# The last pair of graphs in two halves, and the last attentions in a shorter schedule: a graph network on one core

## Chip, core and metric

The kernel runs on one core of a Trainium2 chip. The metric is the device time of one execution in microseconds. The kernel before takes 2255.85 us, the median of three runs (2254.88 to 2256.64).

## What is computed

Sixty-four graphs of 256 nodes with 256 features each. Three GRU layers over the graph (layer 0 of the reference), a residual with a layer norm, then one attention layer with a residual and a layer norm. Everything is fp32.

```python
A = (adj != 0)
h = x
for i in range(3):
    m = einsum('bnd,de->bne', h, weight[i])
    aggr = einsum('bst,bsd->btd', A, m)
    h = gru_cell(aggr, h, w_ih, w_hh, b_ih, b_hh)   # r, z: sigmoid; n: tanh
x = layernorm(x + h)
Wh = x @ W
e = leaky_relu(s1[:, :, None] + s2[:, None, :], 0.2)  # s1, s2: Wh @ a[:F], Wh @ a[F:]
attn = softmax(where(adj > 0, e, -9e15), axis=2)
x = layernorm(x + attn @ Wh)
```

## The kernel before

**Tiles.** Graphs are taken in 32 pairs (`NP`). A pair has 512 node columns (`GN`), so a gate's result fills one PSUM bank of 128x512, and there are eight banks in one pool. The state `hT` is kept transposed, two tiles of 128 features by 512 nodes. To keep fp32 accuracy, an operand of a gate is cut into an upper part H, a rest L and a cross term D (`upper`, `lower`, `cross`, L126 to L134), and a product is a sum over such pieces in two banks, `pga` and `pgb` (L360 to L377): ScalarE evicts the first, VectorE adds the second.

**Blocks.** One layer of one pair is a block: `front` (L290) prepares the pieces of h (`hH`, `hL`, `hD`) and of the aggregation (`hi`, `lo`, then `pa`, then `aH`, `aL`, `aD`); `gates` (L356) makes eight products of r, n, z and t, four for each half `e` of the features, and the elementwise steps of the GRU: the sigmoids and the tanh on ScalarE (L386), two multiplications, a subtraction and an addition on GpSimd (L394, L395, L400, L404), the last addition into `hT` on VectorE (L407). A block's gates are 72 matmuls of 512 columns. The three layers of different pairs are interleaved: with each turn, a new pair starts layer 0, the pair before it does layer 1, and the one before that does layer 2 (L549 to L551). The last six blocks are (31,0), (30,1), (29,2), then (31,1), (30,2), then (31,2).

**Order of the work.** Each engine runs its instructions in the order in which the program issues them. That order is set by a clock of ticks: `at(t, step)` files a step, and `tick()` after every six gate matmuls (L370, L376) runs what has come due, so the steps of the front of the next block and of the attention of earlier pairs fall between the gate matmuls. A block has twelve ticks. The front's steps have fixed offsets, `CLOSE` or `LOOSE` (L545, L546). After the last block the loop at L591 runs the remaining steps in order of their ticks.

**Attention.** After a pair's third layer `attention` (L441) files its steps at offsets up to 72 ticks: load x back (`vT`, 5), join with h (14), transpose and copy (15 to 18), statistics for the first layer norm (23), power on GpSimd (26), shift (28), projection `pwh` (31 to 34) and its spreading with the norm's factor onto `s1`, `s2` and `wh` (32 to 35, half on ScalarE, half on VectorE), transposes of the row scores `s` (36), scores on ScalarE (37), mask (38), maximum (39), exponentials (46, 47), first norm applied to `v` (49, 50), transposes of the weights (53), combine `po` (57, 58), add (58, 59), second norm (61 to 70) and the store (72). The exponential and the sigmoid with tanh sit in different function tables of ScalarE, and the compiled program has a table load wherever one follows the other: 61 in all.

**Rooms.** `room` (L255) gives the large attention tiles: from a pool of their own up to pair 29, and from the tags of the gate pieces (`hH`, `hD`, `aH`, `aD`) for pairs 30 and 31. The tiles `hi` and `lo` have one buffer each, and the s2 tile of the attention uses the buffer of `hi0`. A copy of x (transposed) is put away in DRAM (`stash`, L311) and loaded again for the attention.

Of the kernel before, what the change touches and what calls it, by code (L numbers as in the profile page):

```python
# [17 lines left out]
P = 128  # L18
# [7 lines left out]
def kernel(  # L26
# [91 lines left out]

    def nodes(t, d):

        return t.rearrange("p g c d -> p (g c) d")[:, :, d * P:(d + 1) * P]
# [130 lines left out]

    pairs = {}

    def room(kind, shape, p):  # L255


        name = f"{kind}_{p}"
        if p < NP - 2:
            return late.tile(shape, F32, tag=kind, name=name, bufs=2 if kind == "v" else 1)  # L260
        tag = {"v": "hH", "vT": "hD", "wh": "aH", "sc": "aD"}[kind]
        return work.tile(shape, F32, tag=tag, name=name)

    def to_T(src, dst, d):

        pt = bank("pt")
        for k in range(K):
            nc.tensor.transpose(pt[:, k * P:(k + 1) * P], src[:, k // C, k % C, d * P:(d + 1) * P], ident)  # L268
        after(1, lambda: evacuate(dst[:, d, :], pt))

    def from_T(hT, d):
        pt = bank("pt")
        for k in range(K):
            nc.tensor.transpose(pt[:, k * P:(k + 1) * P], hT[:, d, k * P:(k + 1) * P], ident)  # L274
        return pt

    def begin(p):

        s = pairs[p] = Pair()
        s.x, s.adj = loaded.pop(p), loaded_adj.pop(p)  # L280
        s.A = work.tile([P, G, C, N], F32R, tag="A", name=f"A_{p}", bufs=3)
        nc.vector.tensor_scalar(s.A, s.adj, 0.0, None, op0=ALU.not_equal)
        s.hT = work.tile([P, C, GN], F32, tag="hT", name=f"hT_{p}", bufs=4)

# [5 lines left out]
    def front(p, i, t, pace):  # L290

        nm = f"{p}_{i}"
        hi, lo, src = [None] * C, [None] * C, [None] * C

        def turn(d):
            s = pairs[p]
            if i == 0:
                src[d] = nodes(s.x, d)
                to_T(s.x, s.hT, d)
            else:  # L300
                src[d] = from_T(s.hT, d).rearrange("p (k n) -> p k n", k=K)

        def split(d):
            hi[d] = work.tile([P, K, P], F32R, tag=f"hi{d}", name=f"hi{d}_{nm}", bufs=1)
            nc.scalar.copy(hi[d], src[d])

        def rest(d):
            lo[d] = work.tile([P, K, P], F32R, tag=f"lo{d}", name=f"lo{d}_{nm}", bufs=1)
            lower(nc.gpsimd if i == 0 else nc.vector, lo[d], src[d], hi[d])

        def stash():  # L311
            s = pairs[p]
            s.far = far.tile([P, C, GN], F32, tag="xT", name=f"xT_{p}")
            nc.sync.dma_start(s.far, s.hT)
        if i == 0:
            at(t + pace[0][1] + 2, stash)

        def h_upper():
            s = pairs[p]
            s.hc = pieces(work, [P, C, GN], nm, "h")  # L320
            upper(flat(s.hc[0]), flat(s.hT))

        def h_lower():
            s = pairs[p]
            lower(nc.gpsimd, flat(s.hc[1]), flat(s.hT), flat(s.hc[0]))

        def h_cross():
            s = pairs[p]
            cross(flat(s.hc[2]), flat(s.hT), flat(s.hc[0]))

        def aggregate(d):
            s = pairs[p]
            if d == 0:
                s.ag = pieces(work, [P, C, GN], nm, "a")
            pt = src[d] = bank("pa")
            for g in range(G):
                todo = [(h[d], c) for c in range(C) for h in (hi, lo)]
                for n, (h, c) in enumerate(todo):
                    nc.tensor.matmul(pt[:, g * N:(g + 1) * N], h[:, g * C + c, :], s.A[:, g, c, :],  # L339
                                     start=(n == 0), stop=(n == len(todo) - 1))  # L340

        def a_upper(d):
            upper(pairs[p].ag[0][:, d, :], src[d])

        def a_rest(d):
            H, Lo, Di = [t[:, d, :] for t in pairs[p].ag]
# [9 lines left out]
    def gates(p, i, lags):  # L356

        s = pairs[p]

        def product(dst, o, parts, bias=None):  # L360
# [5 lines left out]
            step = len(todo) // len(parts)  # L366
            for n, (pt, w, m, d) in enumerate(todo):
                nc.tensor.matmul(pt, w[:, d, o * P:(o + 1) * P], m[:, d, :],  # L368
                                 start=n in (0, ends + 1), stop=n in (ends, len(todo) - 1))
                if (n + 1) % step == 0 and n + 1 < len(todo):  # L370
# [5 lines left out]
            tick()  # L376
            nc.vector.scalar_tensor_tensor(dst, b, -1.0 / U, dst, op0=ALU.mult, op1=ALU.add)  # L377

        for e in range(C):
            nm = f"{p}_{i}_{e}"  # L380

            def temp(tag, bufs=2):
                return work.tile([P, GN], F32, tag=tag, name=f"{tag}_{nm}", bufs=bufs)
# [4 lines left out]
            hid, inp = (whh, s.hc), (wc[i], s.ag)  # L388
            bo = [b_sum[:, e:e + 1], b_sum[:, C + e:C + e + 1]]
            r, n, z, t = temp("r", 1), temp("n", 3), temp("z"), temp("t")  # L390
            h = s.hT[:, e, :]
# [4 lines left out]

            product(r, e, [hid, inp])
            after(1, lambda r=r, b=bo[0]: gate(r, AF.Sigmoid, b))
            product(n, 2 * C + e, [hid], bh[:, 2 * C + e:2 * C + e + 1])
            after(2, lambda r=r, n=n: nc.gpsimd.tensor_mul(n, n, r))  # L400
            product(z, C + e, [hid, inp])
            after(2, lambda z=z, b=bo[1]: gate(z, AF.Sigmoid, b))
            product(t, 2 * C + e, [inp])
            after(1, lambda n=n, t=t: nc.gpsimd.tensor_add(n, n, t))  # L404
# [4 lines left out]
    def layer_norm(v, name, t, then=None):  # L409
# [10 lines left out]
        def power():  # L420
            nc.gpsimd.tensor_scalar(rs, mv[:, :, 1], EPS, None, op0=ALU.add)
            nc.gpsimd.tensor_tensor(rs, rs, half, ALU.pow)

        def shift():
            nc.vector.scalar_tensor_tensor(nm, mv[:, :, 0], -1.0, rs, op0=ALU.mult, op1=ALU.mult)
# [5 lines left out]
        for k in range(K):  # L431
            at(t[0] + k // 2, lambda k=k: stats(k))
        at(t[1], power)
        at(t[2], shift)
        for k in range(K):
            at(t[3] + k // 2, lambda k=k: apply(k))
# [4 lines left out]
    def attention(p, t):  # L441

        s = pairs[p]
        pts = {}

        def again():
            s.vT = room("vT", [P, C, GN], p)
            nc.sync.dma_start(s.vT, s.far)
        at(t + 5, again)
        at(t + 14, lambda: nc.vector.tensor_add(flat(s.vT), flat(s.vT), flat(s.hT)))  # L450

        def back(d):
            if d == 0:
                s.v = room("v", [P, G, C, D], p)
            pts[d] = from_T(s.vT, d)
        for d in range(C):
            at(t + 15 + d, lambda d=d: back(d))
            at(t + 17 + d, lambda d=d: nc.vector.tensor_copy(
                nodes(s.v, d), pts[d].rearrange("p (k n) -> p k n", k=K)))
        at(t + 18, lambda: setattr(s, "rs", layer_norm(s.v, f"a_{p}", (t + 23, t + 26, t + 28, t + 49))))  # L460

        def project(k):
            if k == 0:
                s.wh = room("wh", [P, G, C, D], p)
                s.s1 = work.tile([P, K], F32, tag="s1", name=f"s1_{p}")
                s.s2 = work.tile([P, K, P], F32, tag="hi0", name=f"s2_{p}", bufs=1)
            pts[k] = bank("pwh")
            for d in range(C):
                nc.tensor.matmul(pts[k][:, :D + 2], s.vT[:, d, k * P:(k + 1) * P], gw[:, d, :],  # L469
                                 start=(d == 0), stop=(d == C - 1))  # L470

        def spread(k):
            rs = s.rs[:, k:k + 1]
            for dst, src in ((s.s1[:, k:k + 1], pts[k][:, D:D + 1]),
                             (s.s2[:, k, :], pts[k][:, D + 1:D + 2].to_broadcast([P, P])),
                             (s.wh[:, k // C, k % C, :], pts[k][:, :D])):
                if k < 2:
# [3 lines left out]
        for k in range(K):  # L481
            at(t + 31 + k, lambda k=k: project(k))
            at(t + 32 + k, lambda k=k: spread(k))

        def rows():
            pts[0] = bank("s2")
            for k in range(K):
                nc.tensor.transpose(pts[0][:, k * P:(k + 1) * P], s.s2[:, k, :], ident)  # L488

        def scores():  # L490
            s.sc = room("sc", [P, K, N], p)
            for k in range(K):
# [130 lines left out]
```

## Time and profile before

| what | value |
| --- | --- |
| median of three runs | 2255.85 us |
| profiled execution | 2255.94 us |
| its span, first to last instruction | 2254.2 us |
| granted TensorE clock, mean | 0.991 |
| TensorE busy | 2205.3 us, 98% of the span |
| VectorE, ScalarE, GpSimd busy | 1627.0, 1494.6, 1496.7 us |
| TensorE busy in the first 60 us | 45.4 us |
| last gate matmul ends (start of the row transposes behind it) | 2189.24 us |
| last ScalarE row ends | 2250.3 us |

The profile is of one execution; its time is 1.7 us above its span. Busy time counts overlapping rows once. TensorE's matmuls are pipelined, so a matmul's own duration (about 0.4 us for 512 columns) is longer than the distance from one to the next; the chain view, which gives the pieces of the path that ended last, has the distances (four matmuls in 0.93 us). An idle time with an arrow names what the engine waited for.

### The profile page before, as it was taken

The numbers are of one execution on the slowest core, as the hardware profiler recorded it, in microseconds if no ns is written. First come the engines' busy times: TensorE is split into PE (matmuls) and PEld (weight loads), VectorE is DVE, ScalarE is ACT, GpSimd is POOL, SyncE is SP. The second block draws the span as 40 slices with busy tenths as digits, with TensorE's granted clock in tenths as the row PEclk, the third lists the DMA queues.
The fourth block names the chain that finished last, engine by engine and source line by source line (L and its number), as shares of the span: only waits on it lengthen the run. The fifth ranks groups of instructions, "written<-read, shape, count | busy, mean of one in ns | idle before, by whom it ended". The sixth has DMA issues, their size and how long they took to land.

```text
span 2254.2 us, 31118 instructions
## 1 busy us (share of the span) xinstructions
PE 2205.3 (98%) x10980; PEld 1839.0 (82%) x10980; DVE 1627.0 (72%) x2856; ACT 1494.6 (66%) x2771; POOL 1496.7 (66%) x1084
## 2 busy tenths in 40 slices
PE   7999999999999999999999999999999999999985
PEld 5788888888888888888888888888888888888874
DVE  4767777777767777767777767777767777767775
ACT  4556667666667666667666677666677666677664
POOL 5777666676666676666667666667666667666661
PEclk9999999999999999999999999999999999999997
DMA  3001011100011101011101011101011101010000
GB/s 112 29 29 38 28 39 48 47 31 36 34 42 48 47 29 38 30 46 47 47 29 37 29 47 47 48 29 38 29 48 47 47 29 38 29 47 29 20 28 28
DMA packets 62650, 88.50 MB, mean 39 GB/s; under 512 B 2784, under 2 KB 54240, under 8 KB 62496
## 3 DMA queue, kind: packets, MB, share of 16 engines
q1 hardware_dynamic: 60704, 84.68, 10.7%
q8 instruction: 87, 1.43, 0.3%
q10 hardware_dynamic: 1616, 1.57, 0.2%
q14 instruction: 67, 0.55, 0.1%
q0 software_dynamic: 176, 0.27, 0.1%
HBM read 52.96 MB, written 33.55 MB: 38 GB/s over the span
## 4 chain that ended last, share of the span: by engine, by line
PE 95%; DVE 1%; ACT 1%; POOL 1%; issue 1%; DMA 1%; SPq 0%; POOLq 0%; ACTq 0%; DVEq 0%
PE pga L368 47%; PE pgb L368 23%; PE pa L339 8%; PE po L525 5%; PE pwh L469 5%; PE pt L274 4%; PE pt L268 1%; PE pt L517 1%; DMA adj<-in_adj_dram 1%; PE s L488 1%; PE pw L229 0%; ACT v L429 0%; DVE sc L502 0%; DVE st_b L417 0%; POOL wc2L_wc L145 0%
## 5 line engine op out<-in xcount | busy, mean ns | idle before, releaser
L394 POOL TENSOR_TENSOR t<-hT,n 128x512 f32<-128x512 f32 x192 | 255.0, 1328 | 534.3 <-ACT n L386 534.2
L368 PE MATMUL pga<-hH,whhH_whh 128*128 128x512 f32 x1152 | 397.4, 426 | 0.0
L368 PE MATMUL pgb<-hD,whhD_whh 128*128 128x512 f32 x1152 | 361.9, 395 | 0.3 <-DVE hD L134 0.3
L368 PE MATMUL pga<-hL,whhL_whh 128*128 128x512 f32 x1152 | 362.0, 395 | 0.0
L404 POOL TENSOR_TENSOR n<-n,t 128x512 f32<-128x512 f32 x192 | 251.8, 1311 | 114.2 <-DVE t L377 101.2
L377 DVE SCALAR_TENSOR_TENSOR r<-pgb,r 128x512 f32<-128x512 f32 x192 | 131.8, 686 | 254.0 <-PE pgb L368 188.5
L400 POOL TENSOR_TENSOR n<-n,r 128x512 f32<-128x512 f32 x192 | 306.2, 1595 | 0.6 <-DVE n L377 0.4
L395 POOL TENSOR_TENSOR t<-t,z 128x512 f32<-128x512 f32 x192 | 263.1, 1370 | 15.0
L368 PEld LDWEIGHTS pgb<-hD,whhD_whh 128*128 128x128 f32 x1152 | 216.3, 188 | 52.6 <-DVE hD L134 0.8
L368 PEld LDWEIGHTS pga<-hL,whhL_whh 128*128 128x128 f32 x1152 | 216.7, 188 | 51.4
L373 ACT ACTIVATE r<-pga 128x512 f32<-128x512 f32 x192 | 115.2, 600 | 216.0 <-PE pga L368 206.2
L375 ACT ACTIVATE n<-pga,bh 128x512 f32<-128x512 f32 x192 | 131.7, 686 | 164.6 <-PE pga L368 164.5
L131 POOL TENSOR_TENSOR hL<-hT,hH 128x1024 fp32r<-128x1024 f32 x96 | 230.6, 2402 | 7.1 <-ACT hH L128 7.1
L368 PEld LDWEIGHTS pga<-hH,whhH_whh 128*128 128x128 f32 x1152 | 193.9, 190 | 20.8
L339 PE MATMUL pa<-A,hi 128*128 128x256 f32 x768 | 200.4, 293 | 0.0
L373 ACT ACTIVATE z<-pga 128x512 f32<-128x512 f32 x192 | 114.7, 597 | 128.7 <-PE pga L368 128.7
L339 PE MATMUL pa<-A,lo 128*128 128x256 f32 x768 | 192.7, 283 | 4.3 <-POOL lo L131 4.3
L377 DVE SCALAR_TENSOR_TENSOR t<-pgb,t 128x512 f32<-128x512 f32 x192 | 131.8, 686 | 78.3 <-ACT t L373 72.3
L377 DVE SCALAR_TENSOR_TENSOR z<-pgb,z 128x512 f32<-128x512 f32 x192 | 131.9, 687 | 73.7 <-ACT z L373 60.9
L131 DVE TENSOR_TENSOR aL<-pa,aH 128x512 fp32r<-128x512 f32 x192 | 131.6, 685 | 55.4 <-ACT aH L128 55.4
L128 ACT ACTIVATE aH<-pa 128x512 fp32r<-128x512 f32 x192 | 115.1, 600 | 78.5 <-PE pa L339 78.5
L377 DVE SCALAR_TENSOR_TENSOR n<-pgb,n 128x512 f32<-128x512 f32 x192 | 131.8, 686 | 43.7 <-ACT n L375 39.3
(133 smaller groups left out, 5439.6 us busy)
## 6 DMA issues: line engine op xcount, KB each, us to landing
x<-in_x_dram SPq DMA_DIRECT2D x32, 512.0 KB, 4.0
adj<-in_adj_dram SPq DMA_DIRECT2D x32, 512.0 KB, 4.0
xT<-hT SPq DMA_DIRECT2D x32, 512.0 KB, 2.6
vT<-xT SPq DMA_DIRECT2D x32, 512.0 KB, 4.8
out_dram<-v SPq DMA_DIRECT2D x32, 512.0 KB, 2.9
w_n<-in_L_gnn_weight_dram ACTq DMA_DIRECT2D x3, 256.0 KB, 10.4
rows_hH<-in_L_gnn_w_hh_dram SPq DMA_DIRECT2D x1, 512.0 KB, 5.5
rows_aH<-in_L_gnn_w_ih_dram ACTq DMA_DIRECT2D x1, 512.0 KB, 6.0
```

Source lines behind the costliest of these rows:

```text
L128: nc.scalar.activation(dst, src, AF.Copy, scale=1.0 - 2.0 ** -13)
L131: eng.tensor_sub(dst, src, hi.bitcast(F32))
L339: nc.tensor.matmul(pt[:, g * N:(g + 1) * N], h[:, g * C + c, :], s.A[:, g, c, :], start=(n == 0), stop=(n == len(todo) - 1))
L368: nc.tensor.matmul(pt, w[:, d, o * P:(o + 1) * P], m[:, d, :], start=n in (0, ends + 1), stop=n in (ends, len(todo) - 1))
L373: nc.scalar.activation(dst, a, AF.Copy, scale=1.0 + U)
L375: nc.scalar.activation(dst, a, AF.Identity, scale=1.0 + U, bias=bias)
L377: nc.vector.scalar_tensor_tensor(dst, b, -1.0 / U, dst, op0=ALU.mult, op1=ALU.add)
L394: nc.gpsimd.tensor_sub(t, h, n)
L395: nc.gpsimd.tensor_mul(t, t, z)
L400: after(2, lambda r=r, n=n: nc.gpsimd.tensor_mul(n, n, r))
L404: after(1, lambda n=n, t=t: nc.gpsimd.tensor_add(n, n, t))
L469: nc.tensor.matmul(pts[k][:, :D + 2], s.vT[:, d, k * P:(k + 1) * P], gw[:, d, :], start=(d == 0), stop=(d == C - 1))
```

## The change

- A class `Unit` stands for a whole pair or one graph of it; `front`, `gates`, `layer_norm` and `attention` take a unit, and their column ranges come from it. Pairs 0 to 30 are whole units. Pair 31 is two units, 31g0 and 31g1, each with 256 columns. They share `hT`, `A`, the mask and the DRAM copy of x; each has its own pieces and its own attention.
- The last blocks become (31g0,0), (31g1,0), (30,1), (29,2), then (31g0,1), (31g1,1), (30,2), then (31g0,2), (31g1,2).
- A tick is now counted by columns, so that a half block has six ticks. While a half block runs, the front of the next block has the offsets `SHORT`, which fit into six ticks, for a whole pair too; half blocks have shorter lags for tanh, blend and the last addition.
- The attention's offsets become a table; its entries are, in order: again, join, back, v, stats, power, shift, apply, project, rows, scores, mask, max, exp, turn, combine, stats2, power2, shift2, apply2. Up to pair 27 it is the old one (`EVEN`); pair 28 has `BRISK` (56 ticks), pairs 29, 30 and both halves of 31 have `FAST` (35 ticks). With the last two, `s2` lies in the buffer of x.
- `room` takes the gate pieces' tags for pair 31 alone; pair 30 uses the attention's own pool.
- The store of x to DRAM is issued in `h_upper`, in the same tick as before, one issue for each half of pair 31.

```diff
-    def room(kind, shape, p):
-        name = f"{kind}_{p}"
-        if p < NP - 2:
+    def room(kind, shape, u):
+        name = f"{kind}_{u.name}"
+        if u.p < NP - 1:
             return late.tile(shape, F32, tag=kind, name=name, bufs=2 if kind == "v" else 1)
...
         def h_upper():
+            if i == 0:
+                nc.sync.dma_start(u.cols(u.pair.far), u.cols(u.pair.hT))
...
-                nc.tensor.matmul(pt, w[:, d, o * P:(o + 1) * P], m[:, d, :],
+                nc.tensor.matmul(u.bank(pt), w[:, d, o * P:(o + 1) * P], u.col(m, d),
                                  start=n in (0, ends + 1), stop=n in (ends, len(todo) - 1))
-                if (n + 1) % step == 0 and n + 1 < len(todo):
+                done[0] += u.n1 - u.n0
+                step = done[0] % (3 * C * GN) == 0
+                if step and n + 1 < len(todo):
                     tick()
...
     CLOSE = (5, 5, 5, 7, 8, 8), (6, 6, 7)
+    SHORT = (0, 1, 1, 3, 4, 4), (3, 3, 4)
     LOOSE = (2, 3, 4, 6, 7, 8), (5, 8, 10)
+    EVEN = 5, 14, 15, 17, 23, 26, 28, 49, 31, 36, 37, 38, 39, 46, 53, 57, 61, 64, 66, 70
+    BRISK = 5, 14, 15, 17, 19, 21, 23, 32, 23, 28, 29, 30, 31, 33, 37, 41, 45, 48, 50, 54
+    FAST = 2, 5, 6, 7, 9, 10, 12, 22, 14, 18, 19, 20, 20, 22, 25, 27, 30, 31, 33, 33
...
+    units = [Unit(p, 0, G) for p in range(NP - 1)]
+    ends = [Unit(NP - 1, g, g + 1) for g in range(G)]
     blocks = []
     for turn in range(NP + L - 1):
-        blocks += [(turn - i, i) for i in range(L) if 0 <= turn - i < NP]
+        if turn >= NP - 1:
+            blocks += [(u, turn - NP + 1) for u in ends]
+        blocks += [(units[turn - i], i) for i in range(L) if 0 <= turn - i < NP - 1]
...
-            front(np_, ni, clock[0], CLOSE if n and np_ == blocks[n - 1][0] else LOOSE)
+            front(nu, ni, clock[0], CLOSE if n and nu is blocks[n - 1][0] else LOOSE if u.whole else SHORT)
...
-        gates(p, i, (2, 3, 5) if n + 2 >= len(blocks) or blocks[n + 2][0] == p else (4, 5, 10))
+        close = n + 2 < len(blocks) and blocks[n + 2][0] is u or n + 1 < len(blocks) and not blocks[n + 1][0].whole
+        gates(u, i, (1, 2, 4) if not u.whole else (2, 3, 5) if close else (4, 5, 10))
         if i == L - 1:
-            attention(p, clock[0])
+            attention(u, clock[0], EVEN if u.p < NP - 4 else BRISK if u.p < NP - 3 else FAST)
```

## The prediction

> **What bounds the kernel now.** I read the page first, then the busy time by stretches of the last 80 us, then the chain and the timeline there.
>
> ```profile
> span 2254.2 us, 31118 instructions
> PE 2205.3 (98%) x10980; PEld 1839.0 (82%) x10980; DVE 1627.0 (72%) x2856; ACT 1494.6 (66%) x2771; POOL 1496.7 (66%) x1084
> ```
>
> TensorE (PE) is the bound. Of its 48.9 us of idle time the start has about 14.5. The stretches (columns: length, PE, PEld, DVE, ACT, POOL busy, granted PE clock, DMA share, GB/s) show where the rest is:
>
> ```profile
> 2150.00:2175.00 25.00, 24.77 (x125) 20.62 (x124) 21.96 (x44) 12.83 (x21) 15.96 (x12) 1.00 0.06 22
> 2175.00:2190.00 15.00, 14.68 (x67) 11.84 (x65) 8.07 (x16) 9.35 (x20) 9.28 (x9) 1.00 0.03 11
> 2190.00:2200.00 10.00, 1.09 (x8) 0.86 (x8) 7.80 (x16) 7.50 (x19) 4.87 (x4) 0.75 0.28 88
> 2200.00:2210.00 10.00, 8.88 (x40) 8.22 (x41) 5.13 (x12) 2.08 (x7) 2.14 (x2) 0.74 0.01 2
> 2220.00:2230.00 10.00, 4.44 (x14) 3.14 (x15) 5.38 (x11) 9.23 (x29) 0.00 (x0) 0.50 0.15 52
> 2240.00:2254.20 14.20, 3.34 (x9) 2.31 (x8) 3.91 (x13) 3.06 (x7) 1.27 (x2) 0.62 0.21 74
> ```
>
> Up to 2190 PE is full. Then comes a drain in which no engine is full and PE's granted clock falls to between 0.50 and 0.75 in the stretches shown. The chain has its pieces:
>
> ```profile
> 2188.78 0.46 PE pgb L368 x2
> 2189.24 0.45 PE s L488 x4
> ...
> 2195.00 6.12 issue
> ...
> 2228.39 5.75 PE po L525 x16
> ...
> 2237.93 5.42 PE po L525 x16
> ...
> 2249.29 0.98 ACT v L429 x2
> ```
>
> The last gate matmul ends at 2189.24; from there to 2254.2 are 65.0 us of drain: the rest of the attention of pair 29, all but the load of 30, all of 31, each engine taking the three in one order. A last view, ScalarE (ACT) around one softmax in the full part:
>
> ```profile
> 2139.04 0.69 ACT L375 ACTIVATE n<-pga,bh 128x512 f32<-128x512 f32 x1
> 2140.36 1.28 ACT L507 ACT_TABLE_LOAD   x1
> 2142.65 0.58 ACT L373 ACTIVATE z<-pga 128x512 f32<-128x512 f32 x1
> 2145.70 1.28 ACT L386 ACT_TABLE_LOAD   x1
> 2146.99 0.72 ACT L386 ACTIVATE z<-z,b_sum 128x512 f32<-128x512 f32 x1
> ```
>
> Two table loads frame the exponentials, the z eviction starts 3.6 us after the n eviction, and PE isn't held: eight PSUM banks, two for a product, are the cover.
>
> [...] the sigmoid starts at 2146.99, 0.01 us after the load. I use 1.28. [...] The trace has 1.31 us for 512 columns and 2.40 for 1024, a slope of 1.09 per 512, so half width should take about 0.77; no run here shows it. [...] So an eviction waits behind whatever the program put ahead of it. The trace agrees: every row starts in program order.
>
> **The change, part by part.** Up to block (28,2) the instruction order is the same on PE, ACT and POOL. On DVE a reciprocal of 0.17 us comes one tick later, still four ticks ahead of its use: nothing.
>
> *Half-width products.* 216 gate matmuls of 512 columns become 432 of 256. In the chain view four of 512 take 0.93 us (0.2328 each), eight of 256 (the aggregation) 0.95 (0.119). 216 x (2 x 0.119 - 0.2328) = +1.1 us on PE.
>
> *Work moved ahead of the drain.* Row by row from the instruction order, at full clock, the old drain held on PE 40 + 12 transposes (0.11 each), 8 projections (0.87) and 6 combines (1.73): 5.7 + 7.0 + 10.4 = 23.1 us. The new one holds 32 transposes, 8 projections and 4 combines: 3.5 + 7.0 + 6.9 = 17.4. So 5.7 us of attention go in front. Without stalls the last gate matmul ends at 2189.2 + 1.1 + 5.7 = 2196.0.
>
> *Stalls that it adds.* I followed the queues by hand with the durations above, DVE and ACT spaced 0.1 us closer than their durations as in the timeline.
> (a) Blocks (31g0,0), (31g1,0). In the first, ACT has the scores (4 x 0.39), then tanh of graph 0 behind POOL: lo, lo, two blends of pair 28 (1.31 and 1.37), hL (1.3), n·r, n+t. That tanh ends about 12 us into a block of 11.0, and behind it wait evictions that the next block's first product reads: 1.5 us. In the second, the exponentials of pair 27 are cut in two by sigmoids: four loads instead of two. aH of (30,1) comes at 27.9 and its cross term at 29.1 after the first block's start; PE gets there at 27.2 with the 1.5 late: together 2.8.
> (b) Block (29,2). Between the evictions of n and of z ACT has two loads, a sigmoid, another load, two exponential pairs and two applies of v: 1.28 + 1.0 + 1.0 + 1.28 + 0.6 + 1.28 + 1.0 + 1.0 = 8.4 + own 0.5, then two more applies before t. The timeline above has 3.6. PE runs out of banks one product into (31g0,1): transposes wait for z's bank 3.9 us, the next products for t's and for late hi pieces: 5.3.
> (c) Block (30,2), exponentials of 29, uncut: t's eviction 1.5 late.
> (d) Block (31g1,1): pair 30's front in half a block; hL (2.4), n·r, a power (1.27) and n+t on POOL ahead of a tanh, and behind it aH: 1.4.
> Sum 11.0. Bounds: 4 (banks and gaps in ACT hide more than I see) and 17. (31g0,1) and (31g0,2) carry 15.8 us of PE work for 11 to 13 on the others and cost nothing; if (b)'s lag lasted into them it is already counted.
>
> *The drain.* In us after the last gate matmul. h of graph 1: eviction and DVE to 0.7, POOL 1.5, tanh 2.05, two POOL blends 3.65, DVE 4.05 (before: 7.8). DVE then does in order half a spread of pair 30 (0.85), the join (0.6), another spread: 6.3; PE's row transposes, ACT's scores (4 x 0.39) 7.9; mask and max of 30 (1.25 + 1.1) 10.3; ACT four exponentials and four applies 14.4, graph 0's scores 15.2; DVE its mask and max 16.6, copy of weights 17.2, adds of pair 30 with graph 1's spread 20.2, four statistics 22.4, graph 0's copy 23.0. Graph 1's scores are done at 20.3, so it follows: mask and max, PE's combine of graph 0 [...] 25.6, its add and statistics 27.6, copy 28.3, graph 1's combine 30.7, add and statistics 32.7, POOL's power 34.0, shift, apply 35.2, and the 3.9 us that lie between the last ACT row and the span's end now: 39.1. With 0.9 for hand-overs: 40. Bounds 37 and 46.
>
> *SP, POOL.* The stash moves from a slot of its own to ahead of h_upper: same tick (5), so SP's order stays; for the halves two issues take the place of one. SP issues pair 29's load behind pair 27's store, which (b) holds back: load lands (4.8) some 6 us before its join. Graph 1's load needs pair 29's store issued and a freed hD slot: due at about 3.5, join at 4.9. Both hidden; a miss would cost its lateness one to one.
>
> *Sum.* 2196.0 + 11.0 + 40 = 2247.0 of span. The profiled execution took 2255.94 for a span of 2254.2, 1.7 more; the median of the runs is 2255.85. So 2248.6 us; I say 2248.5.
>
> **Rivals.**
> B, stalls absorbed (25%): 4 of stalls, drain 39: 2196 + 4 + 39 + 1.7 = 2240.7. For it: PE waited 0.2 us in all of 2090 to 2190, though ACT was queued there too. Against: 8.9 against 3.6 us between evictions.
> C, the gain is given back (22%): late pieces and a false wait between the graphs, which share hT and the mask: stalls 17, drain 42: 2256.7. For it: pair 30's front in six ticks, where it had twelve.
> D, slower (11%), one mechanism: POOL at half width costs nearly what full width does. Place: the n·r and n+t ahead of each tanh in the six half blocks, with ACT's evictions queued behind that tanh. At 1.31 instead of 0.77 four such operations add 2.2 us to a half block, 13 in all: 2196 + 24 + 41.6 + 1.7 = 2263.3. It ends above before plus 0.2% (2260.4) from about 1.26 us an operation. For it: the 128x4 power takes 1.04, so a call has a price. Against: the slope.
> A, as computed (42%): 2244 to 2253.5.
>
> **How the numbers follow.** 0.2%, about what a measurement of this kernel can tell from no change, is 4.5 us: faster is below 2251.3, slower above 2260.4. A is 3/4 faster, 1/4 same; B faster; C 0.85 same, 0.15 slower; D slower. Faster 0.57, same 0.29, slower 0.14. Low end: half of B left out, 2239; high end within C's upper part, 2258.
>
> **What would show it.** Right: last gate matmul near 2207, drain near 40, PE idle a few us at the start of (30,1) and inside (31g0,1), 67 table loads against 61. Wrong (a), (b): PE full through there, end of gates near 2198. Wrong on the drain: PE's two last combines not 5 us apart, or a load of vT that ends an idle stretch. D: POOL rows of 128x256 near 1.3.

## The result, and the profile after

The changed kernel takes 2281.95 us (median of 4 runs, 2279.70 to 2284.44) against 2256.23 for the kernel before on the same chip: 1.0115 times as long, 95% interval 1.0098 to 1.0133. It is slower by 26 us; the forecast was 2248.5, 7 us faster. The profiled execution took 2284.44 us for a span of 2282.7. The head of its page:

```profile
span 2282.7 us, 31757 instructions
PE 2222.1 (97%) x11196; PEld 1857.8 (81%) x11196; DVE 1633.3 (72%) x2914; ACT 1509.7 (66%) x2835; POOL 1501.6 (66%) x1117
```

TensorE is busy 17 us longer and idle 12 us longer (60.6 instead of 48.9). The stretches that answer to those of before (length, PE, PEld, DVE (VectorE), ACT, POOL (GpSimd) busy, granted PE clock, DMA share, GB/s):

```profile
2050.00:2075.00 25.00, 21.75 (x155) 20.00 (x154) 17.11 (x34) 16.66 (x41) 17.13 (x17) 1.00 0.16 53
2075.00:2100.00 25.00, 20.19 (x114) 16.65 (x113) 14.24 (x27) 20.28 (x39) 10.05 (x11) 0.86 0.00 1
2100.00:2125.00 25.00, 25.00 (x125) 21.13 (x124) 18.63 (x44) 11.23 (x24) 13.07 (x11) 1.00 0.00 1
2125.00:2150.00 25.00, 21.08 (x111) 18.41 (x110) 14.40 (x25) 22.84 (x46) 13.43 (x11) 0.86 0.13 43
2150.00:2175.00 25.00, 21.28 (x159) 20.18 (x158) 19.25 (x45) 9.27 (x22) 13.40 (x14) 0.95 0.00 1
...
2225.00:2250.00 25.00, 14.39 (x74) 11.75 (x72) 16.50 (x47) 13.27 (x34) 11.04 (x16) 0.86 0.10 32
2250.00:2282.70 32.70, 18.20 (x59) 12.92 (x59) 14.66 (x44) 14.30 (x39) 4.08 (x8) 0.72 0.10 33
```

Two of them in the kernel before:

```profile
2075.00:2100.00 25.00, 25.00 (x131) 21.08 (x130) 18.21 (x30) 16.65 (x31) 18.77 (x12) 1.00 0.00 1
2125.00:2150.00 25.00, 25.00 (x126) 20.66 (x125) 18.26 (x22) 20.62 (x40) 15.40 (x12) 1.00 0.09 28
```

Only one of the five stretches from 2050 to 2175 has PE full, as all five were before but for 0.23 us, and in three of the four with holes PE's granted clock is lower (0.86, 0.86 and 0.95; before, 1.00 in all five). The chain at the end still has its combines, 6 us apart instead of 10:

```profile
2264.98 3.49 PE po L563 x8
...
2271.14 3.54 PE po L563 x8
```

To compare executions I cut each at two points: the first gate matmul of block (28,2), up to which nothing differs, and the end of the last gate matmul. Between them lies the *stretch*, behind them the *drain*. (Up to the first point the profiled executions of all kernels here differ by 2.3 us, 2031.9 to 2034.2, without system; so spans aren't compared.) Before, the stretch is 156.3 us (2032.8 to 2189.1, where the next row of PE starts) and the drain 65.1. After, it is 196.5 (2034.2 to 2230.7) and 52.0. So the drain gave 13.1 us, and the stretch took 40.2. Of these, 6.8 were foreseen as work (1.1 for half widths, 5.7 moved out of the drain); the other 33.4 are stalls, where the prediction had 11.0.

What PE waited for in the stretch (line and releaser: us in total, times, longest):

```profile
PE pgb L390 <- DVE aD L130: 4.1, 2, 3.4
PE pt L298 <- ACT z L397: 3.9, 1, 3.9
PE pga L390 <- DVE r_31g L402: 3.0, 1, 3.0
PE pgb L390 <- ACT r_31g L397: 2.5, 1, 2.5
PE pgb L390 <- ACT n_31g L399: 2.4, 3, 1.1
...
```

With the smaller ones they add up to 21.1 us; before, all waits of PE in its stretch were 0.2 us. The other 12.3 us of the stalls lie in matmuls that stand further apart than at full speed. Two of the waits, followed back. At 2085.01, at the end of block (31g1,0), ACT's rows, then POOL's, then PE's:

```profile
2076.02 1.06 ACT L124 ACTIVATE hH<-hT 128x1024 fp32r<-128x1024 f32 x1
2080.27 0.39 ACT L397 ACTIVATE r_31g<-pga 128x256 f32<-128x256 f32 x1 [3.19 <-POOL n_31g L421]
2080.68 1.28 ACT L545 ACT_TABLE_LOAD   x1
...
2082.97 0.57 ACT L124 ACTIVATE aH<-pa 128x512 fp32r<-128x512 f32 x1
```

```profile
2077.16 2.39 POOL L127 TENSOR_TENSOR hL<-hT,hH 128x1024 fp32r<-128x1024 f32 x1 [2.01 <-ACT hH L124]
2079.50 0.74 POOL L421 TENSOR_TENSOR n_31g<-n_31g,r_31g 128x256 f32<-128x256 f32 x1
```

```profile
2085.01 0.77 PE L390 MATMUL pgb<-aD_31g,wc0D_wc 128*128 128x256 f32 x2 [3.42 <-DVE aD L130]
```

ACT does nothing for 3.19 us: the tile `r` has one buffer, so the eviction of r waits until the n·r before it has read the old r; that n·r stands on POOL behind hL of the whole pair 30, which the short front puts into this half block. Behind the eviction on ACT stand a table load, two exponentials and aH, then on DVE aL and aD, and PE waits for the bank that aD frees. At 2174.12 it is another queue. PE's row, then DVE's, then POOL's:

```profile
2174.12 1.22 PE L390 MATMUL pga<-hH,whhH_whh 128*128 128x512 f32 x2 [3.02 <-DVE r_31g L402]
```

```profile
2170.39 1.22 DVE L130 SCALAR_TENSOR_TENSOR hD<-hH,hT 128x1024 fp32r<-128x1024 f32 x1
2171.53 0.42 DVE L444 BATCH_NORM_STATS2 st_b<-v 128x6 f32<-128x256 f32 x1
...
2173.66 0.40 DVE L402 SCALAR_TENSOR_TENSOR r_31g<-pgb,r_31g 128x256 f32<-128x256 f32 x1
```

```profile
2173.84 0.23 POOL L448 TENSOR_SCALAR rs_a<-mv_a 128x4 f32<-128x4 f32 x1 [5.58 <-DVE mv_a L445]
2174.15 1.04 POOL L449 TENSOR_TENSOR rs_a<-rs_a,half 128x4 f32<-128x4 f32 x1
2175.14 0.74 POOL L427 TENSOR_TENSOR n_31g<-n_31g,t_31g 128x256 f32<-128x256 f32 x1
```

PE waits for DVE to add r's second bank. That addition stands behind aL, aD, hD and four statistics of two norms (pair 28's second, pair 29's first); from 2169.19 to 2174.06 DVE has no idle time. The same statistics hold POOL: it stands 5.58 us at the power of pair 29's norm. Behind that waits n + t, and behind n + t on ACT the tanh (6.36 us), n's eviction and aH, for which PE waits only 0.71 us more, at 2177.33.

### The profile page after: what moved, and what is told of

The parts are those of the page before. It is cut to its first block, busy times and chain, and to the rows that moved or that the text cites. A ratio compares the mean times of both kernels' runs of the same rounds, so it can differ in the third digit from the quotient of the medians.

```text
span 2282.7 us, 31757 instructions
## 1 busy us (share of the span) xinstructions
PE 2222.1 (97%) x11196; PEld 1857.8 (81%) x11196; DVE 1633.3 (72%) x2914; ACT 1509.7 (66%) x2835; POOL 1501.6 (66%) x1117
## 3 DMA queue, kind: packets, MB, share of 16 engines
q8 instruction: 89, 1.46, 0.3%
## 4 chain that ended last, share of the span: by engine, by line
PE 93%; ACT 2%; DVE 2%; POOL 1%; issue 1%; DMA 1%; SPq 0%; POOLq 0%; ACTq 0%; DVEq 0%
PE pga L390 45%; PE pgb L390 23%; PE pa L359 8%; PE po L563 5%; PE pwh L506 5%; PE pt L298 4%; PE pt L326 1%; PE pt L555 1%; DMA adj<-in_adj_dram 1%; PE s L525 1%; ACT v L457 0%; ACT sc L545 0%; PE pw L225 0%; ACT L545 0%; POOL hL L127 0%
## 5 line engine op out<-in xcount | busy, mean ns | idle before, releaser
L430 POOL TENSOR_TENSOR t<-hT,n 128x512 f32<-128x512 f32 x186 | 245.9, 1322 | 512.7 <-ACT n L411 512.4
L390 PE MATMUL pga<-hH,whhH_whh 128*128 128x512 f32 x1116 | 386.1, 427 | 3.4 <-DVE r_31g L402 3.0
L390 PE MATMUL pga<-hL,whhL_whh 128*128 128x512 f32 x1116 | 351.8, 396 | 0.0
L390 PE MATMUL pgb<-hD,whhD_whh 128*128 128x512 f32 x1116 | 350.9, 395 | 0.0
L427 POOL TENSOR_TENSOR n<-n,t 128x512 f32<-128x512 f32 x186 | 241.9, 1300 | 122.8 <-DVE t L402 96.4
L421 POOL TENSOR_TENSOR n<-n,r 128x512 f32<-128x512 f32 x186 | 296.4, 1593 | 7.4 <-ACT r L411 7.3
L431 POOL TENSOR_TENSOR t<-t,z 128x512 f32<-128x512 f32 x186 | 255.7, 1375 | 14.6
L390 PEld LDWEIGHTS pgb<-hD,whhD_whh 128*128 128x128 f32 x1116 | 210.1, 188 | 50.3
L127 POOL TENSOR_TENSOR hL<-hT,hH 128x1024 fp32r<-128x1024 f32 x93 | 223.2, 2399 | 10.4 <-ACT hH L124 10.4
L359 PE MATMUL pa<-A,hi 128*128 128x256 f32 x744 | 194.0, 293 | 0.0
L402 DVE SCALAR_TENSOR_TENSOR z<-pgb,z 128x512 f32<-128x512 f32 x186 | 127.9, 688 | 77.5 <-ACT z L397 65.1
```

What stands on the lines that cost most here:

```text
L127: eng.tensor_sub(dst, src, hi.bitcast(F32))
L390: nc.tensor.matmul(u.bank(pt), w[:, d, o * P:(o + 1) * P], u.col(m, d), start=n in (0, ends + 1), stop=n in (ends, len(todo) - 1))
L430: nc.gpsimd.tensor_sub(t, h, n)
L431: nc.gpsimd.tensor_mul(t, t, z)
```

## The experiments

Theory H: the stalls come from the half blocks, whose queues on POOL and ACT hold PE. Theory P: they come from the shorter paces of attention, which crowd exponentials and table loads. The runs, with stretch, PE's marked idle time in it, drain, and the median time:

| kernel | stretch | PE idle | drain | us |
| --- | --- | --- | --- | --- |
| before | 156.3 | 0.2 | 65.1 | 2256 |
| changed | 196.5 | 21.1 | 52.0 | 2281.95 |
| e1 paces alone | 172.8 | 6.2 | 57.4 | 2263.8 |
| e2 halves alone | 184.6 | 15.5 | 68.7 | 2286.2 |
| e5 exponentials together | 193.6 | 20.1 | 49.0 | 2277.2 |
| e6 hL on VectorE | 190.7 | 19.1 | 51.4 | 2277.3 |
| e7 two rooms for r | 192.3 | 20.2 | 51.8 | 2279.5 |
| e8 waits filled | 196.1 | 15.0 | 51.7 | 2282.5 |
| e9 = e6 + e7 | 193.1 | 18.6 | 51.9 | 2278.6 |
| e12 = e9 + later tanh | 188.9 | 16.6 | 52.2 | 2276.7 |
| e13 = e12 + later powers | 187.6 | 15.5 | 48.4 | 2270.7 |
| e14 = e2 + edits of e12 | 175.5 | 11.9 | 68.1 | 2278.0 |
| e18 rooms for norm factors | 197.4 | 20.7 | 51.4 | 2283.5 |
| e4 whole pair, pace of 30, 31 | 158.5 | 1.4 | 59.4 | 2254.4 |
| e11 halves in last layer only | 165.5 | 5.2 | 53.3 | 2254.6 |
| e15 = e11 + two rooms for r | 165.3 | 6.2 | 53.4 | 2254.6 |
| e16 = e11 + hL on VectorE | 165.0 | 4.5 | 54.4 | 2253.5 |
| e17 = e16 + later join | 160.0 | 2.0 | 56.1 | 2251.25 |

### Paces alone, halves alone (e1, e2)

```diff
-    units = [Unit(p, 0, G) for p in range(NP - 1)]
+    units = [Unit(p, 0, G) for p in range(NP)]
```

> Pair 31 stays whole, block order as before; only the new attention paces (pair 28 in 56 ticks, 29, 30 and 31 in 35) are kept. Theory H (the 35 us that the gates lose come from the half blocks, whose POOL and ACT queues hold PE): the last gate matmul ends at 2196 to 2200, the drain is about 55 (h of a whole pair comes later than that of a graph), the time 2252 to 2257, no slower than before. Theory P (they come from the shorter paces, which crowd exponentials and their table loads into few blocks): the gates still end at 2215 or later and the time is above 2270.

In this run pair 29's join reads h ahead of the last addition of its third layer, since a whole block's last addition comes ten ticks after its gates and the join five. So it computes with an unfinished h; the instructions are the same, but what the right order would cost isn't measured.

Ratio 1.0035 (1.0022 to 1.0049). The drain's PE work is that of the changed kernel (8 projections, 4 combines, 32 transposes: 17.4 us), so the stretch without stalls would be 156.3 + 5.7 = 162.0; it is 172.8. Paces alone cost 10.8 us of stalls, more than H allowed and less than P.

```diff
-EVEN if u.p < NP - 4 else BRISK if u.p < NP - 3 else FAST
+EVEN if u.p < NP - 1 else FAST
```

> Pair 31 in two halves with the changed block order, but the attention of pairs 28 to 30 at the old pace; only the two graphs of 31 have the short one. (Pair 30's wh tile lies in the free adjacency buffer.) The old pace leaves far more of pair 30 to the drain, so the time says little; the end of the gates tells. Without stalls it would be near 2190. H: stalls remain but for the cut exponentials of pair 28, 25 to 30 us, so the last gate matmul ends at 2213 to 2222. P: below 2200.

(The small tiles s1, nm and sm have four rooms there.) Without stalls the stretch would be 156.3 + 1.1 = 157.4; it is 184.6. Halves alone cost 27.2. The two together (38.0) are a little more than the 33.4 of the changed kernel: the halves are the larger part, the paces are a part. Some waits need both. The one at 2174.12, with its statistics of pairs 28 and 29 in a half block, has no counterpart in this run.

### What holds ACT in half blocks (e6, e7, e9, e12, e14)

```diff
-            lower(nc.gpsimd, u.cols(u.hc[1]), ...
+            lower(nc.vector if slim else nc.gpsimd, u.cols(u.hc[1]), ...
```

> The changed kernel, but a front that is prepared while a half block runs takes its lower piece of h (hL) on VectorE instead of GpSimd. Theory Q (within H: hL of 1.7 to 2.4 us stands on POOL ahead of n times r, r has one buffer, so its next eviction on ACT waits for that, with everything queued behind it): the waits at 2067.8 and 2085 and part of the one at 2174 go, some 7 us of waiting and 4 us of slow clock behind them, time 2268 to 2275. If the single buffer of r or the table loads are what matters, or VectorE is as full: within 4 us of the changed kernel.

```diff
-            r = temp("r", 1)
+            if u.whole:
+                r = temp("r", 1)
+            else:
+                if u.n0 == 0 and e == 0:
+                    twin[0] = work.tile([P, GN], F32, tag="r", name=f"r_{nm}", bufs=1)
+                r = twin[0][:, e * N:(e + 1) * N]
```

> The changed kernel, but in half blocks r has two rooms: the tile's 512 columns are used in turn by the two feature halves, so that the eviction of r need not wait for the n times r before it. Theory Q: the waits of ACT for n times r (4.0 at 2063, 3.2 at 2077, 3.4 at 2165) go, so does most of what PE waits at 2067.8 and 2085; the n plus t ahead of tanh still waits for hL and, at 2170, for the power: time 2268 to 2276. If hL's length itself or the tables are the cause: within 4 us of the changed kernel.

Both edits:

> Both edits together: hL on VectorE while half blocks run, and two rooms for r in half blocks. Alone they brought the end of the gates from 2231 to 2223.7 and 2225. Theory Q (both cut the same chain, hL ahead of n times r ahead of the eviction of r): little more than the better of the two, gates end at 2220 to 2223, time 2274 to 2277. If each takes away a wait of its own: about 2217.5, time 2270 to 2272.

The stretch falls by 5.8, 4.2 and, with both, 3.4 us; the medians by 4.6, 2.5 and 3.4 us. The two edits do not add: they cut the same chain. But each time falls short of its forecast (2268 to 2275, 2268 to 2276, 2274 to 2277), and the waits of ACT for POOL tell why. In the changed kernel up to the last gate matmul:

```profile
ACT r_31g L397 <- POOL n_31g L421: 13.2, 5, 4.0
ACT n_31g L411 <- POOL n_31g L427: 12.2, 4, 6.4
```

and with both edits:

```profile
ACT n_31g L413 <- POOL n_31g L434: 18.6, 6, 8.5
```

The wait at r's eviction is gone, and the tanh that stands some instructions later takes half of it over. In the kernel before, all waits of ACT for POOL in its stretch are those of the first line here, two at a tanh; but over its whole span r's eviction waited for n·r too, as the second line has it:

```profile
ACT n L386 <- POOL n L404: 3.1, 2, 2.2
```

```profile
L373 ACT ACTIVATE r<-pga 128x512 f32<-128x512 f32 x192 | 115.2, 600 | 216.0 <-PE pga L368 206.2 <-POOL n L400 6.7 <-PE pgb L368 1.6
```

These 6.7 us are five waits of 1.07 to 2.15 us between 88 and 188 us. So the single buffer could be seen at full width, far from the stretch that the change touches.

```diff
-        gates(u, i, (1, 2, 4) if not u.whole else ...
+        gates(u, i, ((1, 2, 4) if i == L - 1 else (2, 3, 5)) if not u.whole else ...
```

> The kernel with hL on VectorE and two rooms for r, and besides tanh, blends and last addition of the half blocks of layers 0 and 1 one tick later (2, 3 and 5 instead of 1, 2 and 4). Theory S (in half blocks ACT is held by POOL at two places, at the eviction of r behind n times r and at tanh behind n plus t; in the changed kernel 13.2 and 12.2 us, and the two rooms alone only moved it to tanh, 20.8): the waits of ACT for POOL fall below 10 us, and the stretch from the start of block (28,2) to the last gate matmul, 196.5 us in the changed kernel and 193.1 with the first two edits, falls to 180 to 187; time 2266 to 2273. If ACT and VectorE have too much to do in half blocks whatever the order: at least 191, time 2276 or more.

The stretch is 188.9, between the two answers; the time, 2276.7, is the second's. ACT's waits for POOL fell to 14.5 (the longest, 6.7, is the one behind the power), not below 10. The later tanh takes 4.2 us off the stretch and 1.8 us off the time.

The same three edits on e2:

> Halves with the old pace up to pair 30 (184.6 us for the stretch), now with hL on VectorE, two rooms for r and the later tanh. Without any stall the stretch would be 157.4 (156.3 before, and 1.1 for half widths). Theory S (ACT's 21 us behind POOL are most of what halves cost): 168 to 175, time 2270 to 2278 (the drain stays at 68 to 69). If halves cost as much without these waits: 180 or more.

175.5: of the 27.2 us that halves cost alone, the three edits return 9.1, a third (the forecast band ended at 175). Of the 18.1 us that are left, PE's marked waits are 11.9:

```profile
PE pga L394 <- ACT aH L124: 2.9, 2, 1.5
PE pga L394 <- ACT n_31g L403: 2.7, 3, 2.1
PE pga L394 <- DVE aL_31g L127: 2.5, 2, 1.4
PE pgb L394 <- DVE aD L130: 1.6, 2, 0.8
...
```

All but the second line are pieces of the next block's front. That they are late because the front has six ticks instead of twelve is read from the rows; no run here gave a half block a longer front, so it isn't shown.

### Cut exponentials (e5)

```diff
-            at(T["exp"] + j // 2, lambda k=k: exps(k))
+            at(T["exp"] + (j // 2 if pace is EVEN else 0), lambda k=k: exps(k))
```

> The changed kernel, but a pair's four exponentials of pairs 28 and later stand in one tick, so that no sigmoid cuts them in two: two table loads (2.56 us of ACT) less for pairs 28 to 30 each at most. What this tells: the share of the cut exponentials in the wait at 2142 (3.9 us, of which 2.6 are two of the three loads ahead of z's eviction). Expected: that wait falls to about 1.5, the gates end 2 to 4 us sooner, time 2277 to 2281. If the wait only moves: within 1.5 us of the changed kernel.

The wait at 2142 fell from 3.89 to 2.47 and the stretch by 2.9 us, the drain by 3.0; ratio 1.0098 (1.0082 to 1.0113). ACT in the changed kernel at that place, which answers to the rows of before in the prediction:

```profile
2132.38 0.68 ACT L399 ACTIVATE n<-pga,bh 128x512 f32<-128x512 f32 x1
2133.07 1.28 ACT L545 ACT_TABLE_LOAD   x1
...
2136.47 1.28 ACT L411 ACT_TABLE_LOAD   x1
...
2138.50 1.28 ACT L545 ACT_TABLE_LOAD   x1
...
2141.78 0.57 ACT L397 ACTIVATE z<-pga 128x512 f32<-128x512 f32 x1
```

Three loads lie between the evictions of n and z, which start 9.4 us apart (3.6 around the softmax shown of the kernel before).

### Is it the clock? (e8)

Behind each of the three waits of 3 us or more (3.42, 3.89 and 3.02 us) the matmuls run at about half speed: after 2142 pairs of 256 columns stand 0.43 us apart instead of 0.238, until some 6 us after the restart, with a granted clock of 0.50 from 2142 to 2148; after 2085 and 2174 pairs of 512 columns stand 0.85 us apart instead of 0.47. Counted against full-speed distances this is 2.2 us after 2085, 3.0 after 2142 and 3.7 after 2174, 8.9 in all of the 12.3 that aren't marked waits. Theory C: these 8.9 us are a cost of their own.

```diff
+                for _ in range(4):
+                    for n in range(ends + 1):
+                        pt, w, m, d = todo[n]
+                        nc.tensor.matmul(u.bank(pt), w[:, d, o * P:(o + 1) * P], u.col(m, d),
+                                         start=n == 0, stop=n == ends)
```

> The changed kernel with TensorE kept at work in three of its waits: ahead of the ones at 2085, 2142 and 2174 the matmuls or transposes that stand there are repeated with the same result (3.8, 4.0 and 3.1 us of repeats), so nothing that is computed changes and no wait is removed. Theory C (a wait of about 3 us or more lowers the granted clock, and the 5 to 8 us behind it run at half speed, 8.9 us in all at these three places): the last gate matmul ends 5 to 9 us sooner though 10.9 us of matmuls were added, time 2273 to 2277. If the clock does not depend on the wait, or ACT and POOL set the time behind it anyway: no sooner, 2280 to 2285.

(The 16 matmuls ahead of 2085 take 1.9 us at full speed, not 3.8.) The fill does what it should at the second place. The changed kernel behind its wait, and then this one:

```profile
2143.73 0.63 PE L390 MATMUL pga<-hL_31g,whhL_whh 128*128 128x256 f32 x2
2144.15 0.63 PE L390 MATMUL pgb<-hD_31g,whhD_whh 128*128 128x256 f32 x2
2144.58 0.63 PE L390 MATMUL pga<-hH_31g,whhH_whh 128*128 128x256 f32 x2
```

```profile
2143.10 0.40 PE L402 MATMUL pga<-hL_31g,whhL_whh 128*128 128x256 f32 x2
2143.34 0.40 PE L402 MATMUL pga<-aH_31g,wc1H_wc 128*128 128x256 f32 x2
...
2145.43 0.50 PE L402 MATMUL pgb<-hD_31g,whhD_whh 128*128 128x256 f32 x2 [1.02 <-ACT n_31g L411]
```

Full speed, and 2 us later PE waits for ACT again. The stretch is 196.1 instead of 196.5, the time the same (2282.5). At the other two places PE waited for aH of the next block even so (1.46 and 1.78 us). So theory C is tested at the second place alone, the one that kept full speed, and fails there: behind the wait the changed kernel's granted clock is low (0.50), but ACT sets the time, and a faster PE only waits for it. What the slow rows cost at the other two stays open.

### The powers' place, the norm's rooms (e13, e18)

```diff
-    FAST = 2, 5, 6, 7, 9, 10, 12, 22, 14, 18, 19, 20, 20, 22, 25, 27, 30, 31, 33, 33
+    FAST = 2, 5, 6, 7, 9, 11, 12, 22, 14, 18, 19, 20, 20, 22, 25, 27, 30, 32, 33, 33
```

> The run with later tanh, two rooms for r and hL on VectorE (stretch 188.9 from the start of block (28,2) to the last gate matmul, 2276.7), and the powers of the short pace one tick later (11 and 32 instead of 10 and 31), so that on POOL n plus t does not stand behind a power that waits for VectorE's statistics. Theory N (that order holds tanh 6.7 us at the wait near 2169, and h of graph 1 some 3 us in the drain): the stretch falls by 3 to 5, the drain by 1 to 3, time 2269 to 2273. If the statistics themselves are late, because VectorE is: within 2 us of 2276.7.

Time 2270.7, 6 us less than e12; the drain is 3.8 shorter, the stretch only 1.3. ACT's waits for POOL in the stretch are now 6.1 us of the 25.4 at the start, and still 187.6 - 163.1 = 24.5 us of stalls are there: 19.3 us of these waits gone gave 8.9 us of stretch. At 2171 PE waits 2.9 us, as in e12 and much as in the changed kernel at 2174.12 (3.02), for DVE, whose queue holds the same statistics. So the power on POOL wasn't what held PE there. In the drain the power's place counts: h of graph 1 is done 7.4 us after the last gate matmul; it was 10.0 in e12 and is 10.0 in the changed kernel, whose POOL shows the same order as at 2174:

```profile
2231.93 0.23 POOL L448 TENSOR_SCALAR rs_a<-mv_a 128x4 f32<-128x4 f32 x1 [2.92 <-DVE mv_a L445]
2232.24 1.04 POOL L449 TENSOR_TENSOR rs_a<-rs_a,half 128x4 f32<-128x4 f32 x1
2233.25 0.72 POOL L427 TENSOR_TENSOR n_31g<-n_31g,t_31g 128x256 f32<-128x256 f32 x1
```

```diff
-tag="rs_" + name[0], name=f"rs_{name}")
+tag="rs_" + name[0], name=f"rs_{name}", bufs=4 if name[0] == "a" else None)
...
-tag="nmr_" + name[0], name=f"nmr_{name}")
+tag="nmr_" + name[0], name=f"nmr_{name}", bufs=4 if name[0] == "a" else None)
```

> The changed kernel with four rooms instead of two for the first norm's factors (rs, nmr). In its drain POOL stands 12.4 us until ACT has applied pair 30's first norm, because graph 1's factor needs the room of pair 30's, and graph 1's spread, scores and softmax come behind. If that sets the end: drain 2 to 4 us shorter (51.7 to about 49), time 2278 to 2280; the gates end as they did. If pair 30's own chain on VectorE sets it: within 1 us.

The second answer, nearly: graph 1's factor comes 3.7 us sooner (2249.9 instead of 2253.65), but the drain is 51.4 instead of 52.0 and the time no better. DVE takes graph 1's last spread behind pair 30's first addition in both kernels (at 2259.27 here, 2259.55 there).

### What can be kept (e4, e11, e15, e16, e17)

With pair 31 whole as in e1, and before's rooms:

```diff
-EVEN if u.p < NP - 4 else BRISK if u.p < NP - 3 else FAST
+EVEN if u.p < NP - 2 else FAST
```

> Pair 31 whole, blocks and rooms as before, the old pace up to pair 29, the short one for pairs 30 and 31 only. The gates should end within 1.5 us of before (2189 to 2191), since nothing new falls between them but pair 30's first steps. Theory D (the drain lasts as long as pair 31's own chain, which the short pace takes first): drain 55 to 60, time 2247 to 2253. If it is the sum of three pairs' work on ACT and VectorE that fills it: 63 to 66, time as before.

The stretch costs 2.2 us and the drain gives 5.7 (in a profiled execution of 2252.0, 2.4 below the median of 13); the time is 0.9995 (0.9987 to 1.0003), no difference that can be told.

```diff
-        if turn >= NP - 1:
-            blocks += [(u, turn - NP + 1) for u in ends]
-        blocks += [(units[turn - i], i) for i in range(L) if 0 <= turn - i < NP - 1]
+        blocks += [(units[turn - i], i) for i in range(L) if 0 <= turn - i < NP]
+    blocks[-1:] = [(u, L - 1) for u in ends]
```

> Pair 31 whole in its first two layers and in two halves only in the third, block order as before; old pace up to pair 29, short pace for pair 30 and the two graphs. Theory H: the stalls of the four half blocks of layers 0 and 1 are gone, those inside the last two blocks (4.7 us in the changed kernel) remain at most, gates end at 2192 to 2197; the drain is 48 to 58 (h of a graph comes sooner, but pair 29's rest lies in it), time 2243 to 2255. If half blocks stall wherever they stand: gates end past 2203 and no gain over before.

(Pair 30's attention tiles lie in the free buffers of x, adj and A, and the norm factors have more rooms.) Stretch 165.5, drain 53.3, ratio 0.9992 (0.9984 to 1.0000): the halves' shorter drain is there, and their stalls, some 8 us, eat it.

With the edit of e7:

> Halves in the last layer only, as in the run before of that kind (gates end 165.5 us after the start of block (28,2), drain 53.3, 2254.6), and two rooms for r in them. There ACT stood 3.4 us at the eviction of r behind n times r, and aL, aD, the last addition of pair 30 and its join came late behind it (PE waited 3.8). Theory S: the stretch falls to 161 to 163, drain as it was, time 2250 to 2253. If tanh takes the wait over: no gain, 2254 to 2256.

No gain: tanh took the wait over, as in e9.

With the edit of e6:

> Halves in the last layer only, and hL of the second graph on VectorE instead of GpSimd, so that n times r has nothing ahead of it on POOL. Theory S: 3 to 4 us less up to the last gate matmul, time 2250 to 2252. If VectorE, which has the join of pair 30 and the pieces to do there, is late instead: no gain.

0.9988 (0.9982 to 0.9995), but the stretch moved by 0.5 only; PE still waits 3.76 us for the join of pair 30, whose h comes late in half blocks.

```diff
+    THEN = 2, 8, 9, 10, 12, 14, 15, 22, 15, 19, 20, 21, 21, 23, 25, 27, 30, 32, 33, 33
...
-EVEN if u.p < NP - 2 else FAST
+EVEN if u.p < NP - 2 else THEN if u.p < NP - 1 else FAST
```

> Halves in the last layer alone with hL on VectorE (2253.5), the join of pair 30 and its transposes three ticks later (8 to 10 instead of 5 to 7; it still has its scores one tick after the old place), powers one tick later. The wait of TensorE for that join (3.8 us, inside the last two blocks) goes: stretch 161 to 162 instead of 165.0. If the drain (54.4) is then no longer: time 2249 to 2251. If pair 30 comes later in the drain for it: no gain, 2253 to 2255.

(`FAST` has its two powers one tick later here, as in e13, so the join and the powers aren't told apart.) 2251.25, ratio 0.9979 (0.9972 to 0.9987): faster than both kernels, by 0.2% of the one before. The stretch is 160.0, PE idle in it 2.0; the drain grew by 1.7, a part of what was saved. Its last stretches:

```profile
2175.00:2194.30 19.30, 17.75 (x132) 16.53 (x131) 13.54 (x32) 12.12 (x34) 13.47 (x17) 1.00 0.05 15
2194.30:2250.40 56.10, 30.76 (x126) 23.44 (x124) 35.78 (x100) 28.73 (x76) 10.70 (x18) 0.76 0.13 42
```

## Why the prediction was wrong

The miss in figures: stalls 33.4 instead of 11.0, drain 52.0 instead of 40, together 34.4; 2248.6 + 34.4 = 2283.0, and the profiled execution, which came to block (28,2) 1.5 us later than the one of before, took 2284.4.

*The terms that held.* Half-width products stand 0.118 to 0.119 us apart, as the +1.1 us had it. What ACT and DVE take at half width was the author's estimate; the trace has 0.38 us for an eviction of r and 0.51 for its sigmoid on ACT, and 0.41 for the addition of its second bank on DVE (means of 12; at full width before 0.60, 0.73 and 0.69). The instruction order up to (28,2), 67 table loads against 61 and the load of pair 29's vT as hidden were right. The drain held the PE work that the text counted, 32 transposes, 8 projections and 4 combines, 17.4 us at full clock.

*The step that failed: "Stalls that it adds", 11.0 us with bounds 4 and 17.* It was 33.4, nearly twice the upper bound. Of this 21.1 us are marked waits. Term by term:
- (b), 5.3 us: the wait for z's bank in (31g0,1) was put at 3.9 us and is 3.89, at 2142.41; the reading of ACT's queue was right. The share of the cut exponentials in it is 1.4 us (e5). The other 1.4 us of the term aren't there as marked waits.
- (a), 2.8 us: the six waits from 2067.83 to 2089.07 add up to 7.5 us. The prediction had tanh behind POOL as the place. The first to block was r's eviction, one instruction that the text named nowhere: `temp("r", 1)` lets it wait for n·r. In the stretch of before no such wait shows, elsewhere in it 6.7 us do; in the stretch of the changed kernel ACT stands 13.2 us so.
- (c), 1.5 us: t's eviction in block (30,2) holds PE 0.98 us at 2204.94. Kind and place were right.
- (d), 1.4 us: the waits there are 4.4 (0.70, 3.02, 0.71). Only the last lies where the text put it, at aH behind a tanh behind a power on POOL; and that power waits 5.58 us for DVE's statistics, where the text had only its 1.27 us of work. The long wait is for DVE's own queue, which the term left out.
- Blocks (31g0,2) and (31g1,2) had no term beyond (c): three waits of 1.03 to 1.59 us, 3.7 in all.
- The slow matmuls behind waits had none either: 8.9 us by the rows. e8 shows for one of the three places that this isn't a cost to be added, since ACT comes no sooner.

Two sizes carry this: halves alone cost 27.2 us, paces alone 10.8. The prediction had weighed table loads and exponentials (its (a) in part, (b), (c)) above the half blocks' own chain, and that was the wrong way round. It also had followed each stall on its own. That a late piece makes the next block's front late, and that a front in six ticks has no slack in which to catch up, is argued, not shown.

*The drain: 40 us with bounds 37 and 46; 52.0 measured.* h of graph 1 was put at 4.05 us after the last gate matmul and came at 10.0, since pair 30's power stood ahead of its n + t; the chain of POOL in the text started with n + t. e13 gives 3.8 us of drain back by that order alone; h comes at 7.4 there. Behind h come 42.0 us where the text had 36. Most of the difference arises before graph 1's scores, which end 21.7 us behind h (2262.39) where the text had 16.25. On that way the text has no table load ahead of pair 30's exponentials (1.28 us at 2248.22), and it took the projections at full clock (3.5 us for 16 matmuls; the trace has 5.54 at 2236.90, with a granted clock of 0.65). Graph 1's combine takes 3.53 us, with a granted clock of 0.55, where the text has 2.4 (28.3 to 30.7). How much each of these and DVE's order share stays open; e18 excludes the norm factors' rooms, and e5 shows 3.0 us for exponentials in one tick.

*The rivals.* C had the right kind (late pieces, pair 30's front in six ticks) with stalls of 17 and a drain of 42: half of the truth in the stalls. Its false wait between the graphs wasn't tested. D had the right sign and the right place (n·r and n + t ahead of tanh, ACT queued behind), but its price is wrong: the POOL operations of 128x256 took 0.75 to 0.86 us on average, near the 0.77 worked out from 1.31 us for 512 columns and 2.40 for 1024, not 1.26 (by the text's own sums D would need about 1.2). So D's mechanism is false: POOL is slow there because of what stands ahead, not because of width. No rival was slow enough: the slowest, D, ended at 2263.3.

*What stays open.* The hold of POOL on ACT is shown, but for the smaller part: with most of it gone (e13) the stalls fall from 33.4 to 24.5 us. Of what is left the paces alone may explain 10.8 (e1). The rest, late pieces of fronts in six ticks with DVE's statistics between them, is read from rows and not isolated by a run.

## What to carry to other kernels

When a stage is cut in two to pipeline it, follow every tile with one buffer and every in-order queue at the new spacing: waits that don't show there at full width (here r's one buffer, 0 to 13.2 us of ACT in the stretch) appear, and removing one handed half of it to a later instruction in the queue. Read the whole trace of before for them: this one had five, early in the span. In a queue look for the instruction that waits, not only for the sum of the work: a power of 1.3 us held POOL for 5.6. And follow each wait to the engine that ends it: at 2174.12 POOL stood still too, but DVE held PE. Here the split paid only where the drain profits (the last layer), with other work's steps moved later: that version is 0.2% faster than before, where the split in all three layers costs 1.2%.

## What the runs showed of the hardware

- After waits of PE the matmuls often came at half speed for some us (0.43 instead of 0.238 us for a pair of 256 columns, for about 6 us after 2142.41). The length of the last wait doesn't tell when. In the changed kernel it was so behind 3.42, 3.89 and 3.02 us and not behind 2.51 and 0.23 (2067.83, 2069.26); in e2 it was so behind the same 2.51 and 0.23 us (2065.87, 2067.30), in e14 behind 0.93 and 1.11 (2066.20, 2068.41). In e14 the marked idle time ahead of it was 2.0 us within 3.2. At 2142 in e8, repeats of transposes in place of a wait of 3.9 us kept full speed.
- Half-width POOL operations took 0.72 to 0.74 us at best and 0.75 to 0.86 on average, 0.53 to 0.65 of a full one in the same execution. The last addition on DVE of 128x256 took 0.42 us mostly, but 1.30 at 2166.36, while POOL ran hL.
- On ACT, DVE and POOL the rows that write a tile stand in the trace of before in the order in which the program issues them: all 2582, 2855 and 1072.
